# First and last steps in another order, zero matmuls and one small activation during the first loads, in a two-layer graph network kernel

## The chip, the cores and the metric

One NeuronCore of one Trainium2 chip runs the whole program. The metric is device time in microseconds (us); before the change the median of three runs is 1987.33 us. Engines are named as in the profile: PE is TensorE (PEld its weight loads), DVE is VectorE, ACT is ScalarE, POOL is GpSimd, SP is SyncE, which here only issues DMAs. An engine's queue is worked off in order; a `q` after a name (SPq) marks the sequencer that waits or issues.

## The reference

The input x is 128 batches of 128 rows and 512 columns, float32, and adj is a 128 x 128 matrix that is used as weight in layer 0 and as mask in layer 1.

```python
# layer 0: A = adj @ x, C = A + b
pre = A[:, :, None, :] + (C - A)[:, :, :, None]
out = jnp.max(jax.nn.relu(pre), axis=-1)          # = relu(max_n A + b), one number per row
x = _layernorm(x + out)
# layer 1: 8 heads of 64
qkv = x @ w_qkv
attn = softmax(where(adj == 0, -inf, q @ k.T * hd ** -0.5))
o = (attn @ v) @ w_proj + b_proj
x = _layernorm(x + (o + (layernorm(o) * ln_gamma + ln_beta)))
```

## The kernel before

Four batches make a group (32 groups), two batches a pair (64 pairs, called q or p). Per pair: layer 0 takes one 128 x 512 product with adj transposed (`l0_mm`, psum tile pa), a row maximum on DVE (`l0_max`, L267), an addition on ACT (`l0_add`, L272), statistics on DVE and POOL (`bn`, `finish_stats`: bn_stats L235, bn_aggr L236, then a small chain of POOL operations, among them a power, L246 to L248) and a normalization on ACT (`l0_norm`, `normalize`, L254). The result is transposed into x1T: for the first group by PE (`l0_transpose_pe`), for all others by DVE in blocks of 32 (`l0_transpose`) and through DRAM (`l0_write`, `l0_read`: eight DMAs of SP for each pair). `l0_beta` and `l0_spill` put x + beta away for the tail.

The big products (q and k from wqk, v from wv, o from wp) are done by Strassen's scheme in the form with seven products: a `Unit` has products 1 to 7, each of 4 matmuls, which the profile shows as 8 passes, since a float32 matmul is two. Sums of the weight blocks (`weight_sums`, POOL) and of the left blocks (`left_sums`, tiles s_x and s_o; on POOL, for the first group on DVE) feed them. Products 1, 6 and 7 add up in PSUM bank b1, product 2 goes to b2, 5 and 3 to b3, 4 to b4. `snap(k)` copies b1 to SBUF on ACT (u_qk, u_v, u_o, L173), `result(i, j)` adds a snap to a bank on DVE (L179). So product 6 waits for snap 1, product 7 for snap 2, the next unit's product 1 for snap 3, and product 3, which writes b3 after product 5, for result (1, 1).

Attention for batch b: `scores` (PE, psum tiles pss), `softmax_max` (DVE), `softmax_exp` (ACT, eight rows of operations, L400), `softmax_div` and `prob_transpose` (DVE, L411, L413, L421), through DRAM (`prob_write` one DMA, `prob_read` four, tile pT), `attend` (PE, psum po), `attend_copy` (ACT, tile oT, L471).

The tail of a batch, spread over later pairs: normalization of o (`tail_inner`, ACT), three operations on POOL (`tail_residual`: times gamma, plus o, plus the stored x), statistics, normalization (`tail_outer`, ACT) and store (SP). For the last batches there are single-row forms: `tail_inner_one`, `tail_residual_one`, `tail_outer_one`, `last_project` (a plain product with w_proj, psum tile pp), and `tail_fused`, which does inner normalization and residual in three DVE operations (L594 to L596) straight from the statistics.

All instructions are pinned in program order on each engine, so the order of the text is the order of every queue. What runs when is written out by hand: a prologue (from L612) prepares batches 0 to 9 and starts on q and k of the first group, then the loop from L706 runs pairs p = 0 to 60, and the last pairs from L860 on are written out. In the prologue, at L664 to L678, the results of the first unit stand ahead of the "second" statistics (batches 4 to 7), the sums of wv and two of the four normalizations. In the loop at p = 0 there is no attention of an earlier pair to hide behind. In the tail, L is batch 127.

Of the kernel before, what the change touches and what calls it, by code (L numbers as in the profile page):

```python
# [9 lines left out]
F32 = mybir.dt.float32  # L10
AF = mybir.ActivationFunctionType
# [5 lines left out]
def kernel(  # L17
# [30 lines left out]
    nc = tc.nc  # L48
    B, P, D = x.shape
# [3 lines left out]
    G = 4  # L53
    GT = G * P
    HT = GT // 2
    HE = D // 2
# [8 lines left out]
    const = ctx.enter_context(tc.tile_pool(name="const", bufs=1))  # L65
    sb = ctx.enter_context(tc.tile_pool(name="sb", bufs=1))
    small = ctx.enter_context(tc.tile_pool(name="small", bufs=4))
    dram = ctx.enter_context(tc.tile_pool(name="dram", bufs=3, space=bass.MemoryType.DRAM))
    psum = ctx.enter_context(tc.tile_pool(name="psum", bufs=1, space=bass.MemoryType.PSUM))

    pin = tc.keep_in_program_order

    def pe(*args, **kwargs):
        pin(nc.tensor.matmul(*args, **kwargs))  # L74
# [2 lines left out]
        pin(eng.tensor_tensor(dst, a, b, op))  # L77


    adj_sb = const.tile([P, P], F32, name="adj_sb")  # L80
    pin(nc.sync.dma_start(out=adj_sb, in_=adj))
    bias0 = const.tile([P, 1], F32, name="bias0")
# [2 lines left out]
    def broadcast(queue, name, src):  # L85
        t = const.tile([P, D], F32, name=name)
        pin(queue.dma_start(out=t, in_=src.partition_broadcast(P)))
        return t
# [26 lines left out]
    def weight_sums(w, cols, width):  # L115
        t = w[:, :, :, ds(cols, width)]
        b11, b21, b22, b12 = (t[:, i] for i in range(4))
        tt(nc.gpsimd, t[:, 4], b12, b11, ALU.subtract)
        tt(nc.gpsimd, t[:, 6], b22, b12, ALU.subtract)
        tt(nc.gpsimd, t[:, 5], b22, t[:, 4], ALU.subtract)  # L120
        tt(nc.gpsimd, t[:, 3], b21, t[:, 5], ALU.subtract)
# [3 lines left out]
    wv = const.tile([P, 7, 2, HE], F32, name="wv")  # L125
# [7 lines left out]
    weight_load(wqk, w_qkv, 0, D, HE, HE)  # L133
    load(3)

    ident = const.tile([P, P], F32, name="ident")
    make_identity(nc, ident)
    mhalf = const.tile([P, 1], F32, name="mhalf")
# [94 lines left out]
    def bn(src, mv, k):  # L233
        st = small.tile([P, 6], F32, tag="st", name=f"st_{k}_{mv.name}")
        pin(nc.vector.bn_stats(st, src))  # L235
        pin(nc.vector.bn_aggr(mv[:, k], st))  # L236

    def finish_stats(mv, keys):

        n = len(keys)  # L240
        if n == 0:
            return
        sh = small.tile([P, NC], F32, tag="sh", name=f"sh_{mv.name}")
        pin(nc.vector.tensor_scalar(sh[:, :n], mv[:, :n, 0], -1.0, None, ALU.mult))
        rs = small.tile([P, NC], F32, tag="rs", name=f"rs_{mv.name}")
        pin(nc.gpsimd.tensor_scalar(rs[:, :n], mv[:, :n, 1], EPS, None, ALU.add))  # L246
        tt(nc.gpsimd, rs[:, :n], rs[:, :n], mhalf.to_broadcast([P, n]), ALU.pow)
        tt(nc.gpsimd, sh[:, :n], sh[:, :n], rs[:, :n], ALU.mult)  # L248
        for k, key in enumerate(keys):
            stat_of[key] = rs[:, k : k + 1], sh[:, k : k + 1]  # L250
# [23 lines left out]
    def l0_norm(f):  # L274
        normalize(xs[f], xs[f], ("y", f))
# [133 lines left out]
    def softmax_div(b):  # L409
        rec = small.tile([P, H], F32, tag="rec", name=f"rec_{b}")  # L410
        pin(nc.vector.reciprocal(rec, psums.pop(b)))  # L411
        p = prob[b]
        tt(nc.vector, p, p, rec.unsqueeze(2).to_broadcast([P, H, P]), ALU.mult)  # L413
# [38 lines left out]
    def attend(b, tag="po"):  # L452
        g, h, jj = place(b)
        v, t = vs[g, h], pT.pop(b)
        pos[b] = psum.tile([P, NP, P], F32, tag=tag, name=f"po_{b}")
        for pr in range(NP):
            for par in range(2):
                pe(
                    pos[b][ds(par * HD, HD), pr],
                    lhsT=v[:, jj, ds((2 * pr + par) * HD, HD)],  # L460
                    rhs=t[:, :, par * NP + pr],
                    start=True,
                    stop=True,
                )

    def attend_copy(b):
        g, h, jj = place(b)
        if jj == 0:
            tag = "x" if (g, h) == (NG - 2, 0) else "oT"
            oT[g, h] = sb.tile([P, KC, HT], F32, tag=tag, name=f"oT_{g}_{h}", bufs=2)  # L470
        pin(nc.scalar.copy(oT[g, h][:, :, ts(jj, P)], pos.pop(b)))  # L471
# [45 lines left out]
    def o_of(b):  # L517
        g, h, jj = place(b)
        return os_[b] if b in os_ else os_[g, h][:, jj]
# [60 lines left out]
    def tail_inner_one(b):  # L580
        z_tile(b)
        normalize(zs[b], o_of(b), ("o", b))

    def tail_residual_one(b):
        tt(nc.gpsimd, zs[b], zs[b], ga_bc, ALU.mult)
        tt(nc.gpsimd, zs[b], zs[b], o_of(b), ALU.add)
        tt(nc.gpsimd, zs[b], zs[b], rs_.pop(b), ALU.add)

    def tail_fused(b, mean):

        z_tile(b)
        z, o, (rs, _) = zs[b], o_of(b), stat_of.pop(("o", b))
        stt = nc.vector.scalar_tensor_tensor
        pin(stt(z, o, mean, ga_bc, ALU.subtract, ALU.mult))  # L594
        pin(stt(z, z, rs, o, ALU.mult, ALU.add))
        tt(nc.vector, z, z, rs_.pop(b), ALU.add)  # L596

    def tail_outer_one(b):
        z = zs.pop(b)
        normalize(z, z, ("z", b))  # L600
        pin(nc.sync.dma_start(out=out[b], in_=z))

    def stats(name, *items):

        mv = small.tile([P, NC, 2], F32, tag="mv", name=f"mv_{name}")
        for k, (kind, b) in enumerate(items):
            bn({"o": o_of, "z": zs.get, "y": xs.get}[kind](b), mv, k)
        finish_stats(mv, items)
        return mv
# [4 lines left out]
    mv = [small.tile([P, NC, 2], F32, tag="mv", name=f"mv_first_{k}") for k in range(2)]  # L614
# [10 lines left out]
    weight_sums(wqk, HE, HE)  # L625
    for f in range(G):
        l0_norm(f)
    for f in range(2):
        l0_transpose_pe(f)

# [30 lines left out]
    weight_load(wp, w_proj, 0, HE, 0, HE)  # L661
    ga_bc = broadcast(nc.sync, "ga_bc", ln_gamma)
    bp_bc = broadcast(nc.sync, "bp_bc", b_proj)
    before.snap(3)  # L664
    before.result(1, 1)
    before.result(1, 0)
    stats("second", *(("y", f) for f in range(G, 2 * G)))
    weight_sums(wv, 0, HE)
    for f in range(G, G + 2):
        l0_norm(f)  # L670
    cur.product(2)
    cur.product(1)
    cur.snap(1)
    cur.result(0, 0)
    before.product(3)
    before.result(0, 1)
    for f in range(G + 2, 2 * G):
        l0_norm(f)  # L678
    cur.product(6)
    cur.snap(2)  # L680
    cur.product(5)
# [24 lines left out]
    for p in range(LAST + 1):  # L706
        g, ph = divmod(p, 2)
        a, b = 2 * p, 2 * p + 1
        first = v_unit(0) if p == 0 else qk_unit(g + 1, ph)
        n = p + 4 if p + 4 < B // 2 else None  # L710
        f = p + 5 if p + 5 < B // 2 else None
        ta, tb, to = tails(p)
        mv = small.tile([P, NC, 2], F32, tag="mv", name=f"mv_{p}")
        keys = []
# [79 lines left out]
            l0_read(n)  # L794
        if p > 0:
            first.snap(3)
        softmax_div(b)
        prob_transpose(b)
        prob_write(b)
        prob_read(a)  # L800
        prob_read(b)
        first.result(1, 1)
        first.result(1, 0)
        if ph == 1 and tb is not None:
            one("z", zs, tb)
        if ph == 0 and ta is not None:
# [13 lines left out]
        if p == 0:  # L820
            xsums = x_sums(1)
            run_sums(xsums[:3])
            second = qk_unit(1, 0)
        elif p == LAST:
            second = qk_unit(g + 1, 1)
        else:
            second = v_unit(g + 1) if ph else o_unit(g - 1)
# [32 lines left out]
    L = B - 1  # L860
# [101 lines left out]
    o_u.result(0, 0)  # L962
    v_u.product(3)
    v_u.result(0, 1)
    for t in range(L - 11, L - 7):
        tail_residual_one(t)
    o_u.product(6)
    softmax_exp(L, range(4))
# [14 lines left out]
    tail_outer(B // 2 - 7)  # L983
    tail_store(B // 2 - 7)
    mv = small.tile([P, NC, 2], F32, tag="mv", name="mv_last_2")
    keys = [("z", L - 11), ("z", L - 10), ("o", L - 5), ("o", L - 4), ("o", L - 7), ("o", L - 6)]
    bn(zs[L - 11], mv, 0)
    bn(zs[L - 10], mv, 1)
    o_u.result(1, 1)
    o_u.result(1, 0)  # L990
    bn(o_of(L - 5), mv, 2)
    bn(o_of(L - 4), mv, 3)
    o_u.product(3)
    o_u.result(0, 1)
    last_project(L - 3, wlast, "b2")
    last_project(L - 2, wlast, "pss0")
    attend(L - 1)
    attend_copy(L - 1)
    attend(L, "pa")
    attend_copy(L)  # L1000
    last_project(L - 1, wlast, "pss1")
    last_project(L, wlast, "b1")
    bn(o_of(L - 7), mv, 4)
    bn(o_of(L - 6), mv, 5)
    finish_stats(mv, keys)
    for t in (L - 5, L - 4, L - 7, L - 6):
        tail_inner_one(t)
    for t in (L - 11, L - 10):
        tail_outer_one(t)
    tail_residual_one(L - 5)  # L1010
    mv = stats("last_3", ("o", L - 3), ("o", L - 2), ("z", L - 9), ("z", L - 8))
    tail_residual_one(L - 4)
    for t in (L - 9, L - 8):
        tail_outer_one(t)
    tail_fused(L - 3, mv[:, 0, 0:1])
    tail_fused(L - 2, mv[:, 1, 0:1])
    mv = stats("last_4", ("o", L - 1), ("z", L - 3), ("z", L - 2))
    tail_residual_one(L - 7)
    tail_fused(L - 1, mv[:, 0, 0:1])
    for t in (L - 3, L - 2):  # L1020
        tail_outer_one(t)
    mv = stats("last_5", ("o", L), ("z", L - 5), ("z", L - 4))
    tail_residual_one(L - 6)
    tail_fused(L, mv[:, 0, 0:1])
    for t in (L - 5, L - 4):
        tail_outer_one(t)
    stats("last_6", ("z", L - 1), ("z", L - 7))
    stats("last_7", ("z", L), ("z", L - 6))
    for t in (L - 1, L - 7, L, L - 6):
        tail_outer_one(t)  # L1030


# [39 lines left out]
```

## Time and profile before

| What | Value |
|---|---|
| Median of three runs | 1987.33 us (1987.06 to 1987.37) |
| Profiled execution, its own time | 1988.53 us |
| Span of its instructions | 1986.7 us |
| PE busy | 1946.4 us, 98% of the span |
| DVE, POOL, ACT busy | 79%, 65%, 53% |
| Chain that ended last: PE's share | 95% |
| Mean granted TensorE clock | 0.991 |

The profile is of one execution. The span runs from its first instruction to its last; the execution's own time is 1.8 us more. "Busy" of an engine is the sum of its instructions' durations. The granted clock is the share of full speed that the chip allowed TensorE. A line of waits reads: who waited, for whom, us in total, times, longest. A line of the timeline reads: start in us from the span's start, duration, engine, line, operation, output and inputs, shape, count; in brackets the idle time of the engine before it and what ended it. A line of the chain: start, duration, what.

### The profile page before, as it was taken

The page shows a single profiled execution, that of the slowest core. Times are in us where ns is not written, and L with a number is a line of the kernel's source. Part 1 is how long each engine was busy: PE and PEld are TensorE (multiplying, and loading weights), DVE is VectorE, ACT ScalarE, POOL GpSimd, SP SyncE. Part 2 cuts the span into 40 slices and gives each one's busy share as a digit, 9 for nine tenths or more (in the row PEclk, how much of TensorE's full clock was granted, in tenths as well). Part 3 has the DMA queues.
Part 4 walks back from the last instruction along what each step waited for, and adds up shares of the span by engine and source line. Part 5 has one row for each costly group of instructions (what it writes and reads, how often), then busy time and mean ns, then how long its engine had stood idle before and what let it go on. Part 6 is the DMA issues. An engine that isn't in the chain of part 4 may idle for free.

```text
span 1986.7 us, 33036 instructions
## 1 busy us (share of the span) xinstructions
PE 1946.4 (98%) x11545; PEld 1644.8 (83%) x11545; DVE 1565.2 (79%) x2518; ACT 1055.1 (53%) x3066; POOL 1293.7 (65%) x808
## 2 busy tenths in 40 slices
PE   7999999999999999999999999999999999999994
PEld 5888888888888888888888888888888888888872
DVE  5668788788788788787787787787787787787685
ACT  3435546546556556555555555555455455455453
POOL 5246667677667677667676667676667676676646
PEclk8999999999999999999999999999999999999997
DMA  5665576675675675765766765765766766765553
GB/s 191 145 170 139 159 195 155 181 195 153 183 187 158 186 187 157 187 170 169 192 168 169 194 165 164 202 165 164 202 159 168 198 164 165 198 162 158 159 177 121
DMA packets 445655, 341.76 MB, mean 172 GB/s; under 512 B 276912, under 2 KB 378416, under 8 KB 445488
## 3 DMA queue, kind: packets, MB, share of 16 engines
q1 hardware_dynamic: 445056, 338.85, 64.1%
q8 instruction: 92, 1.51, 0.3%
q10 hardware_dynamic: 432, 0.79, 0.1%
q14 instruction: 75, 0.61, 0.1%
HBM read 172.82 MB, written 166.72 MB: 171 GB/s over the span
## 4 chain that ended last, share of the span: by engine, by line
PE 95%; DVE 2%; DMA 1%; POOL 1%; ACT 0%; issue 0%; SPq 0%; ACTq 0%; POOLq 0%; DVEq 0%
PE b_qk L74 39%; PE b_v L74 19%; PE b_o L74 19%; PE pss L74 6%; PE po L74 6%; PE pa L74 5%; PE pp L74 0%; POOL zl L77 0%; DMA x<-in_x_dram 0%; DMA wqk<-in_L_gnn_w_qkv_dram 0%; DVE s_x L77 0%; DMA hop<-pu 0%; DVE st_mv_last L235 0%; DVE z L77 0%; POOL rs_mv_last L77 0%
## 5 line engine op out<-in xcount | busy, mean ns | idle before, releaser
L74 PE MATMUL b_qk<-s_x,wqk 128*128 128x256 f32 x2048 | 476.3, 381 | 4.0 <-ACT u_qk L173 3.9
L74 PEld LDWEIGHTS b_qk<-s_x,wqk 128*128 128x128 f32 x2048 | 391.8, 191 | 58.1 <-POOL wv L77 4.3
L400 ACT ACTIVATE s<-s,nmax 128x128 f32<-128x128 f32 x1024 | 396.2, 391 | 6.7 <-DVE nmax L393 6.7
L74 PE MATMUL b_qk<-x1T,wqk 128*128 128x256 f32 x1536 | 360.7, 385 | 0.8 <-DVE x1T L299 0.8
L74 PEld LDWEIGHTS b_qk<-x1T,wqk 128*128 128x128 f32 x1536 | 288.7, 191 | 45.5 <-DVE x1T L299 1.2
L77 POOL TENSOR_TENSOR z<-z,ga_bc 128x1024 f32<-128x1024 f32 x58 | 164.6, 2838 | 168.4 <-ACT z L254 168.4
L246 POOL TENSOR_SCALAR rs_mv<-mv 128x6 f32<-128x6 f32 (+2 forms) x61 | 14.6, 240 | 380.2 <-DVE mv L236 380.2
L77 DVE TENSOR_TENSOR s<-s,rec 128x1024 f32<-128x1024 f32 x128 | 252.3, 1971 | 4.4
L173 ACT COPY u_qk<-b_qk 128x512 f32<-128x512 f32 x192 | 112.3, 585 | 248.2 <-PE b_qk L74 247.2
L74 PE MATMUL b_v<-wv,s_x 128*128 128x256 f32 x1024 | 237.2, 380 | 2.0 <-DVE v L179 2.0
L74 PE MATMUL b_o<-wp,s_o 128*128 128x256 f32 x992 | 230.2, 380 | 0.5 <-DVE v L179 0.5
L74 PEld LDWEIGHTS b_v<-wv,s_x 128*128 128x128 f32 x1024 | 194.8, 190 | 28.7 <-DVE v L179 2.4
L179 DVE TENSOR_TENSOR qk<-b_qk,u_qk 128x512 f32<-128x512 f32 x256 | 168.1, 675 | 62.2 <-PE b_qk L74 44.6
L381 DVE SCALAR_TENSOR_TENSOR s<-pss,mask 128x512 f32<-128x512 f32 x256 | 164.3, 684 | 59.5 <-PE pss L74 59.1
L74 PEld LDWEIGHTS b_o<-wp,s_o 128*128 128x128 f32 x992 | 188.5, 190 | 26.7 <-DVE v L179 0.9
L77 POOL TENSOR_TENSOR x<-x,be_bc 128x1024 f32<-128x1024 f32 x64 | 182.1, 2847 | 34.0 <-DVE rec L411 27.6
L400 ACT ACTIVATION_READ_ACCUMULATOR s<-s,nmax 128x1 f32 x1024 | 194.2, 190 | 0.0
L179 DVE TENSOR_TENSOR v<-b_v,u_v 128x512 f32<-128x512 f32 x128 | 87.0, 681 | 133.6 <-PE po L74 128.8
L173 ACT COPY u_o<-b_o 128x512 f32<-128x512 f32 x93 | 54.4, 585 | 247.3 <-PE b_o L74 247.3
L173 ACT COPY u_v<-b_v 128x512 f32<-128x512 f32 x96 | 56.2, 585 | 238.5 <-PE b_v L74 238.5
L74 PE MATMUL b_v<-wv,x1T 128*128 128x256 f32 x768 | 176.3, 379 | 0.0
L74 PEld LDWEIGHTS b_v<-wv,x1T 128*128 128x128 f32 x768 | 146.3, 190 | 31.9 <-issue 13.8
(107 smaller groups left out, 3395.5 us busy)
## 6 DMA issues: line engine op xcount, KB each, us to landing
hop<-pu SPq DMA_DIRECT2D x128, 512.0 KB, 3.5
pT<-hop SPq DMA_DIRECT2D x512, 128.0 KB, 3.7
spill<-x SPq DMA_DIRECT2D x64, 512.0 KB, 4.8
x<-in_x_dram SPq DMA_DIRECT2D x62, 512.0 KB, 4.4
xhop<-xt SPq DMA_DIRECT2D x248, 128.0 KB, 2.3
x1T<-xhop SPq DMA_DIRECT2D x248, 128.0 KB, 3.9
xr<-spill SPq DMA_DIRECT2D x59, 512.0 KB, 3.6
out_dram<-xr SPq DMA_DIRECT2D x58, 512.0 KB, 4.1
```

The source lines that it names most:

```text
L74: pin(nc.tensor.matmul(*args, **kwargs))
L77: pin(eng.tensor_tensor(dst, a, b, op))
L173: pin(nc.scalar.copy(t, self.banks[1]))
L179: nc.vector.tensor_tensor(self.out[half, col], self.banks[bank], self.snaps[k], ALU.add)
L246: pin(nc.gpsimd.tensor_scalar(rs[:, :n], mv[:, :n, 1], EPS, None, ALU.add))
L381: nc.vector.scalar_tensor_tensor(s[:, par], pss[b][par], SCALE, mask.unsqueeze(1).to_broadcast([P, NP, P]), ALU.mult, ALU.add,)
L400: nc.scalar.activation(prob[b][:, i], prob[b][:, i], AF.Exp, bias=nmax[b][:, i : i + 1], accum_out=psums[b][:, i : i + 1],)
```

## The change

It has five parts. On each engine the same work is done except for the added operations and, in the tail, two batches (L-4 and L-6) that take the fused form on DVE in place of `tail_inner_one` and `tail_residual_one`; the groups of the last statistics are cut anew.

```diff
+    zeros = const.tile([P, 2 * P], F32, name="zeros")
+    pin(nc.vector.memset(zeros, 0.0))
+    idle = psum.tile([P, 2 * P], F32, tag="b1", name="idle")
+    def keep_warm(n):
+        for _ in range(n):
+            pe(idle, lhsT=zeros[:, :P], rhs=zeros, start=True, stop=True)
...
     load(3)
+    warm = small.tile([P, 1], F32, tag="r", name="warm")
+    pin(nc.scalar.activation(warm, zeros[:, :1], AF.Identity, bias=zeros[:, :1]))
+    keep_warm(3)
     ident = const.tile([P, P], F32, name="ident")
...
     for f in range(G):
         l0_norm(f)
+    keep_warm(5)
     for f in range(2):
         l0_transpose_pe(f)
...
     bp_bc = broadcast(nc.sync, "bp_bc", b_proj)
+    stats("second", *(("y", f) for f in range(G, 2 * G)))
+    weight_sums(wv, 0, HE)
     before.snap(3)
     before.result(1, 1)
     before.result(1, 0)
-    stats("second", *(("y", f) for f in range(G, 2 * G)))
-    weight_sums(wv, 0, HE)
-    for f in range(G, G + 2):
-        l0_norm(f)
     cur.product(2)
     cur.product(1)
     cur.snap(1)
     cur.result(0, 0)
     before.product(3)
+    for f in range(G, 2 * G):
+        l0_norm(f)
     before.result(0, 1)
-    for f in range(G + 2, 2 * G):
-        l0_norm(f)
...
         if p > 0:
             first.snap(3)
+        else:
+            first.result(1, 1)
+            first.result(1, 0)
         softmax_div(b)
         prob_transpose(b)
         prob_write(b)
         prob_read(a)
         prob_read(b)
-        first.result(1, 1)
-        first.result(1, 0)
+        if p > 0:
+            first.result(1, 1)
+            first.result(1, 0)
...
-    for t in range(L - 11, L - 7):
+    for t in range(L - 11, L - 8):
         tail_residual_one(t)
...
-    keys = [("z", L - 11), ("z", L - 10), ("o", L - 5), ("o", L - 4), ("o", L - 7), ("o", L - 6)]
+    keys = [("z", L - 11), ("z", L - 10), ("o", L - 5), ("o", L - 4)]
...
     bn(o_of(L - 5), mv, 2)
     bn(o_of(L - 4), mv, 3)
+    finish_stats(mv, keys)
+    tail_inner_one(L - 5)
+    for t in (L - 11, L - 10):
+        tail_outer_one(t)
+    tail_residual_one(L - 8)
     o_u.product(3)
     o_u.result(0, 1)
     last_project(L - 3, wlast, "b2")
     last_project(L - 2, wlast, "pss0")
     attend(L - 1)
+    attend(L, "pa")
+    mv2 = stats("last_3", ("o", L - 7), ("o", L - 6), ("z", L - 9))
+    tail_inner_one(L - 7)
+    tail_outer_one(L - 9)
+    tail_residual_one(L - 5)
+    tail_fused(L - 4, mv[:, 3, 0:1])
     attend_copy(L - 1)
-    attend(L, "pa")
     attend_copy(L)
     last_project(L - 1, wlast, "pss1")
     last_project(L, wlast, "b1")
-    bn(o_of(L - 7), mv, 4)
-    bn(o_of(L - 6), mv, 5)
-    finish_stats(mv, keys)
-    for t in (L - 5, L - 4, L - 7, L - 6):
-        tail_inner_one(t)
-    for t in (L - 11, L - 10):
+    mv = stats("last_4", ("o", L - 3), ("z", L - 8), ("z", L - 4))
+    tail_residual_one(L - 7)
+    for t in (L - 8, L - 4):
         tail_outer_one(t)
-    tail_residual_one(L - 5)
-    mv = stats("last_3", ("o", L - 3), ("o", L - 2), ("z", L - 9), ("z", L - 8))
-    tail_residual_one(L - 4)
-    for t in (L - 9, L - 8):
+    tail_fused(L - 6, mv2[:, 1, 0:1])
+    mv2 = stats("last_5", ("o", L - 2), ("z", L - 6), ("z", L - 5))
+    tail_fused(L - 3, mv[:, 0, 0:1])
+    for t in (L - 6, L - 5):
         tail_outer_one(t)
-    tail_fused(L - 3, mv[:, 0, 0:1])
-    tail_fused(L - 2, mv[:, 1, 0:1])
-    mv = stats("last_4", ("o", L - 1), ("z", L - 3), ("z", L - 2))
-    tail_residual_one(L - 7)
+    tail_fused(L - 2, mv2[:, 0, 0:1])
+    mv = stats("last_6", ("o", L - 1), ("z", L - 3), ("z", L - 2), ("z", L - 7))
+    for t in (L - 3, L - 2, L - 7):
+        tail_outer_one(t)
+    mv2 = stats("last_7", ("o", L))
     tail_fused(L - 1, mv[:, 0, 0:1])
-    for t in (L - 3, L - 2):
-        tail_outer_one(t)
-    mv = stats("last_5", ("o", L), ("z", L - 5), ("z", L - 4))
-    tail_residual_one(L - 6)
-    tail_fused(L, mv[:, 0, 0:1])
-    for t in (L - 5, L - 4):
-        tail_outer_one(t)
-    stats("last_6", ("z", L - 1), ("z", L - 7))
-    stats("last_7", ("z", L), ("z", L - 6))
-    for t in (L - 1, L - 7, L, L - 6):
+    tail_fused(L, mv2[:, 0, 0:1])
+    stats("last_8", ("z", L - 1), ("z", L))
+    for t in (L - 1, L):
         tail_outer_one(t)
```

In the built program the change shows on the queues as follows. PE: three matmuls with the tile `idle` ahead of the transpose of adj, five ahead of the first `l0_transpose_pe`, and nothing else moved. DVE: one memset at the start, the four "second" statistics ahead of two results, two results of v ahead of the division of batch 1, and a new order in the tail. ACT: one activation behind the table load, the first u_qk copy of the second unit ahead of all four normalizations, and in the tail five activations ahead of the last two oT copies. POOL: six residual operations fewer, and the statistics in smaller groups. SP: the last stores in another order. GpSimd's "second" statistics and sums of wv keep their places on POOL.

## The prediction

> **What bounds the kernel now.** I read the page first, then TensorE's waits, then the granted clock by stretch, then the two ends in order of time. The page, busy time by engine and TensorE's 40 slices:
>
> ```profile
> PE 1946.4 (98%) x11545; PEld 1644.8 (83%) x11545; DVE 1565.2 (79%) x2518; ACT 1055.1 (53%) x3066; POOL 1293.7 (65%) x808
> ...
> PE   7999999999999999999999999999999999999994
> ```
>
> TensorE is the bound everywhere except in the first and the last slice. TensorE's waits from 0 to 80 us, then from 80 to 1936 us:
>
> ```profile
> PE b_qk L74 <- ACT u_qk L173: 3.9, 1, 3.9
> ...
> PE b_v L74 <- DVE v L179: 2.0, 1, 2.0
> ...
> PE b_o L74 <- DVE v L179: 0.5, 1, 0.5
> ```
>
> The loop waits 0.5 us in 1856. So a microsecond saved before 80 us stays saved to the end, and the tail's length adds directly. Granted clock (the column before the DMA share) in stretches I cut where it changes:
>
> ```profile
> 16.90:23.70 6.80, 6.02 (x21) 4.79 (x20) 1.78 (x3) 2.10 (x3) 6.64 (x8) 0.50 0.50 163
> ...
> 44.20:51.00 6.80, 5.72 (x14) 4.59 (x15) 3.69 (x6) 2.94 (x5) 6.72 (x6) 0.50 0.35 83
> ...
> 80.00:1960.00 1880.00, 1878.50 (x11285) 1596.21 (x11285) 1496.86 (x2399) 1019.66 (x2993) 1237.94 (x746) 1.00 0.65 173
> ```
>
> Half clock twice, each time 6.8 us, each time begun inside or just after a pause of TensorE (13.2 to 15.9, 41.3 to 45.3). Before 13.5 the record says 1.00, but six passes of 512 columns from 7.73 took 5.49 us, where eight take 3.70 in the tail: cold as well. The chain of waits around the second:
>
> ```profile
> 41.80 1.03 POOL rs_mv_second L77
> ...
> 43.87 0.80 ACT x L254
> 44.66 0.48 ACT u_qk L173
> 45.28 6.54 PE b_qk L74 x16
> ```
>
> ScalarE had the copy u_qk (L173) queued behind two normalizations (L254) that wait for the "second" statistics; and the 16 passes after it took 6.54 us, where 16 take 3.45 in the loop (6.91 for 32). The timeline at the other cold place, and at the end:
>
> ```profile
> 18.29 3.78 PE L74 MATMUL b_qk<-x1T,wqk 128*128 128x256 f32 x8 [0.78 <-DVE x1T L299]
> ...
> 1952.52 0.58 ACT L471 COPY oT<-po 128x512 f32<-128x512 f32 x1 [10.20 <-PE po L74]
> ...
> 1960.77 1.24 DVE L77 TENSOR_TENSOR z<-z,wlast 128x512 f32<-128x512 f32 x1
> 1961.52 1.12 PE L74 MATMUL pp<-bp_bc,ones 1*128 1x512 f32 x2
> ...
> 1982.83 0.80 ACT L254 ACTIVATE zl<-zl,sh_mv_last,rs_mv_last 128x512 f32<-128x512 f32 x1
> ```
>
> After TensorE's last matmul (1962.6) come 21 us of VectorE, GpSimd and ScalarE in turn, then 3.1 us of store.
>
> **What the Trainium skill says.** "TensorE: Matmul & The Clock Gate", Part 1: the clock is halved by default, rises after a busy window of about 3.4 us, falls after an idle one, and the window runs free. The trace agrees: both cold stretches are 6.8 us, two windows. Its Part 4 says that transposes by TensorE don't count as busy in the same way; the trace agrees insofar as eight transposes at 15.9 did not stop the fall at 16.9. "SBUF — State Buffer", Who interferes with whom: a VectorE operation with two SBUF inputs and a GpSimd operation that reads SBUF exclude each other. The trace agrees: the sums s_x on VectorE took 0.95, 1.64, 1.75 and 2.83 us beside GpSimd's, while operations with a PSUM input took 0.68 to 0.75. "ScalarE: Activation LUTs", What ACT_TABLE_LOAD costs: 1283 ns; the trace has 1.28 at 7.58.
>
> **The change, part by part** (times in the frame of before).
>
> *Three zero matmuls and the small activation at the start.* Six passes of 256 columns, cold 0.47 each (3.78/8): 2.8 us, from about 0.8 (a memset of VectorE comes first, 0.2 to 0.3 by L148 and L150) to 3.6. The adjacency transpose starts at 3.62 when its data land, so at most 0.1 is late; the next matmul that matters waits for x until 7.68. Cost 0. They could lift the clock early, but the window up to about 6.7 would be some 75% busy and no such window lifted it in before (one 69% busy, 6.7 to 10.1, did not): 0, with up to 1.2 to gain. The activation pulls the table load from 7.58 to the start; row addition 0 would be done by 8.3 instead of 9.6, but its reader, VectorE's statistics, stands behind a maximum that waits for TensorE until 9.84: 0.
>
> *Five zero matmuls after the first maxima's products.* Ten passes from 13.2, of which 0.3 us is cold (the clock rises at 13.5), then 0.216 each: done by 15.6. The first transpose waits for ScalarE until 15.91, so the cost is 0; were all ten cold, 13.2+4.7 = 17.9 and 2.0 late. The window 13.5 to 16.9 then is 60% zero matmuls where it was 28% busy. I take it that the clock stays up: the eight passes at 18.29 take 1.73, not 3.78 (2.05), the eight transposes behind them 1.72, not 1.92 (0.2). What is late next: the sums s_x on VectorE, now against GpSimd's weight sums the whole time. The second sum is done by 25.2 to 25.8 where TensorE wants it at 25.2: minus 0.3. Net gain 1.9, between −2 and 3.4.
>
> *"second" statistics and weight sums ahead of the results, normalizations behind product 3.* VectorE runs four statistics (0.83 each) first, at 33.7 to 37.0, and GpSimd has them at about 38.7. The two results (1.29), now behind them, end at 38.5; product 3, which overwrites their bank, begins at 37.7 and needs only the first, done at 37.9: 0.2, inside my rounding. On ScalarE the copy u_qk stands before the normalizations and runs at 37.8 to 38.4; the four normalizations end at 41.8; the next copy (snap 2) waits for them until 41.8, and product 7, its reader, begins at 46.3. So the 3.9 us wait goes, and with it the cold stretch: 6.54−3.45 = 3.1. Behind the normalizations stand transposes, eight writes and eight reads of SP (3.7 and 6.8 us to issue): landed at about 57 where they landed at 60.9; GpSimd's first reader, at 67.9 before, moves to 59.0. Covered by 2; without that cover each microsecond counts. Gain 7.0, between 3 and 7.
>
> *p = 0: results (1,1), (1,0) ahead of the second division.* VectorE idled 1.49 us before that division (waiting for the exponentials, 73.56 to 75.04); the two results (1.25) fit there, and TensorE finds its bank free at 76.4 instead of 78.4: 2.0. What is late next: the eight reads of pT. The last is issued at 82.7 and takes 3.7 to land: 86.45, unmoved by this edit; the second attend would start at 88.2−2.0 = 86.2. Minus 0.3. Gain 1.7.
>
> *The tail.* TensorE's order is the same. Two of the eight GpSimd residuals (three operations of 1.27 us each) become VectorE's fused form; statistics are split into smaller groups. ScalarE's two oT copies (1952.52) now stand behind five activations. These need the statistics of L−7 and L−9: GpSimd does residual L−9 by 1939.95, statistics 1942.6, residual L−8 by 1946.4, statistics 1947.9; the activations end at 1949.5. The copies' input is ready at 1952.5: 3 us of cover, cost 0. After that VectorE is the chain, from 1942.97 on. Statistics: 3+3+3+4+1+2 = 16 at 0.83, and six short ones, about 14.5. Fused on PSUM, four at 0.75+0.75+0.7 to 0.9, 9.5. Fused on SBUF, two: alone 2.1, at GpSimd's pace (three of 1.65) 4.95; GpSimd is half in short operations then, so I take 3.0 and 3.5. Sum 30.5: VectorE ends at 1973.5. Then GpSimd's three short steps 1.3, ScalarE's two rows 1.5: 1976.2 to 1976.6, against 1983.6. The store behind is as before. Gain 7.0; 3.4 for both fused at the worst pace; 9.5 at the best.
>
> **Sum.** 1.9+7.0+1.7+7.0 = 17.6. The profiled execution's span was 1986.7 and its own time 1988.5, 1.2 above the median 1987.33 of the runs. Span 1969.1, its own time 1970.9, median **1969.7 us**.
>
> **Rivals.**
> *The clock does not stay up* (zeros or 60% don't count, or the phase differs): the first 2.2 go, and up to 2.0 for cold zeros: 1972 to 1974. For: the skill on transposes. Against: the second cold stretch is then cured anyway, since no pause is left. 12%.
> *The tail's fused steps run at GpSimd's pace*, or residual L−7 becomes late: gain 3.4, 1973.3. For: s_x at 1.64 to 2.83. Against: most of GpSimd's time there is short operations. 12%.
> *The wait moves*: transposed tiles for the second group come late, and the 3.9 us come back: 1973 to 1980. For: only 2 us of cover. 7%.
> *No net change*: the tail gives nothing and the wait and cold return. Needs two failures: 4%.
> *Slower*: the pT reads. If TensorE, pulled ahead at p = 0, met them late in each of the 61 passes, a wait of 0.35 us a pass would eat 21.6 us. It decides from 0.29 us (17.6/61) on; at 0.5 the time is 2000. For: the loop's reads are the tightest transfer at p = 0 (1.8 us of cover). Against: in the loop the last read is issued by 110.8 and the attend begins at 117.2, 6.4 later, and VectorE idles 6 to 9 us of every 30, so it catches up. 4%.
>
> **Numbers.** The likeliest case has 61%, its own range 1966 to 1973 (clock up early −1.2, fused steps −2.5; s_x and rounding +3). With the clock and tail rivals the range 1965.5 to 1976.5 holds 8 in 10 and more. A difference of 0.2% (4 us) is about what can be told from none: faster 0.92, same 0.04, slower 0.04.
>
> **What would show it.** No wait of 3.9 on u_qk and no half clock at 44 to 51; granted clock 1.00 between 17 and 24; eight passes of b_qk in 1.7 us at about 18.3; no wait on v near 69; the two oT copies still released by TensorE; VectorE without a gap over 0.5 us after the last matmul, and 17 rather than 24 us from there to the end. The prediction is wrong if TensorE shows new waits in the loop, or if the fused steps L−4 and L−6 take over 5 us each.

## The result, and the profile after

The changed kernel takes 1971.99 us in the median of four runs (1970.57 to 1972.82), the kernel before 1987.35 us in four runs beside it (1987.06 to 1988.32): a ratio of 0.9921, interval 0.9904 to 0.9938. That is 15.4 us, or 0.8%, faster. The forecast was 1969.7, range 1965.5 to 1976.5. The profiled execution has a span of 1970.7 us and an own time of 1972.51, so the span is 16.0 us shorter than the one before. In the changed kernel's text the copy of a snap is line 185, a result 191, the statistics 247 and 248, the small chain behind them 256 and 258, normalization 266, the fused steps 606 and 607.

The page's busy time and TensorE's slices:

```profile
PE 1945.3 (99%) x11561; PEld 1642.2 (83%) x11561; DVE 1571.6 (80%) x2526; ACT 1054.3 (53%) x3065; POOL 1289.6 (65%) x805
...
PE   8999999999999999999999999999999999999996
```

Only the first slice (7 to 8) and the last (4 to 6) differ. TensorE's waits from 0 to 80 us, then from 80 to 1936 us:

```profile
PE pt L309 <- ACT x L266: 2.2, 1, 2.2
...
PE b_qk L74 <- DVE v L191: 0.2, 1, 0.2
...
PE b_o L74 <- DVE v L191: 0.5, 1, 0.5
```

The 3.9 us on u_qk and the 2.0 us on v are gone, and the loop has no new wait. The chain of waits where the 3.9 us stood:

```profile
38.71 5.45 PE b_qk L74 x24
44.16 1.72 PE pa L74 x4
45.87 3.45 PE b_qk L74 x16
```

TensorE runs through, 24 passes in 5.45 us at full clock. The granted clock by stretch (the column before the DMA share):

```profile
2.08:5.50 3.42, 3.04 (x7) 1.71 (x7) 0.42 (x2) 1.58 (x2) 0.00 (x0) 1.00 0.77 217
12.32:15.74 3.42, 1.21 (x8) 0.57 (x7) 2.92 (x10) 2.15 (x4) 1.56 (x5) 1.00 1.09 358
15.74:22.57 6.83, 6.05 (x19) 4.82 (x20) 1.67 (x3) 2.10 (x3) 6.67 (x7) 0.50 0.75 255
37.50:44.30 6.80, 6.77 (x31) 5.55 (x30) 5.46 (x11) 4.02 (x6) 6.12 (x7) 1.00 0.73 235
```

The second cold stretch is gone. The first is still there, as long as before: 6.83 us. The timeline of TensorE at the start shows why:

```profile
1.17 2.93 PE L74 MATMUL idle<-zeros 128*128 128x256 f32 x6 [1.17 <-DVE zeros L82]
...
7.79 2.84 PE L74 MATMUL pa<-x,adjT 128*128 128x512 f32 x6 [1.58 <-DMA x<-in_x_dram]
10.47 2.32 PE L74 MATMUL idle<-zeros 128*128 128x256 f32 x10
14.96 1.79 PE L309 MATMUL pt<-ident,x 128*128 128x128 f32 x8 [2.17 <-ACT x L266]
17.52 3.78 PE L74 MATMUL b_qk<-x1T,wqk 128*128 128x256 f32 x8 [0.78 <-DVE x1T L311]
```

The three early zero matmuls did what I had priced at nothing: the clock was up when the six row passes came (2.84 us; 5.49 before). The five later ones did not do what I had priced at 2.2: they ran at full speed, were done at 12.8, and left a gap of 2.17 us. The window from 12.32 is 35% busy (1.21 of 3.42 us), the clock fell at 15.74, and product 1 took 3.78 us as before. Other profiles agree: in all nine of kernels with the early zero matmuls the six row passes take 2.84 us, in the five of kernels without them 4.74 to 5.49; and in all six that have the five later ones and no more, product 1 takes 3.60 to 3.78 us. The tail:

```profile
1935.12 0.94 DVE L256 TENSOR_SCALAR sh_mv_last<-mv_last 128x3 f32<-128x3 f32 x1
...
1941.43 1.28 POOL L77 TENSOR_TENSOR zl<-zl,o 128x512 f32<-128x512 f32 x1
...
1941.56 1.18 DVE L256 TENSOR_SCALAR sh_mv_last<-mv_last 128x3 f32<-128x3 f32 x1
...
1942.11 0.59 ACT L483 COPY oT<-po 128x512 f32<-128x512 f32 x1 [0.46 <-PE po L74]
1942.65 0.74 DVE L606 SCALAR_TENSOR_TENSOR zl<-o,mv_last,ga_bc 128x512 f32<-128x512 f32 x1
1942.79 1.73 POOL L77 TENSOR_TENSOR zl<-zl,wlast 128x512 f32<-128x512 f32 x1
...
1943.49 1.57 DVE L607 SCALAR_TENSOR_TENSOR zl<-zl,rs_mv_last,o 128x512 f32<-128x512 f32 x1
...
1948.11 1.26 POOL L77 TENSOR_TENSOR zl<-zl,o 128x512 f32<-128x512 f32 x1
...
1948.31 1.09 DVE L256 TENSOR_SCALAR sh_mv_last<-mv_last 128x3 f32<-128x3 f32 x1
...
1951.13 1.12 PE L74 MATMUL pp<-bp_bc,ones 1*128 1x512 f32 x2
...
1966.05 1.52 ACT L266 ACTIVATE z<-z,sh_mv_last,rs_mv_last 128x512 f32<-128x512 f32 x2 [4.97 <-POOL sh_mv_last L77]
```

The last matmul ends at 1952.25, the span at 1970.7: 18.46 us, where it was 24.11. The oT copy is still released by TensorE. But three operations of 128 x 3 numbers took about 1 us each, where I had put 0.2. The chain of waits in this stretch names another engine:

```profile
1942.79 1.73 POOL zl L77
1944.51 0.65 POOL rs_mv_last L258
...
1945.25 1.29 POOL rs_mv_last L77
...
1951.01 1.36 POOL rs_mv_last L77
...
1952.40 0.76 DVE z L607
```

By this view GpSimd, not VectorE, is the chain until 1952.37; VectorE's last stretch follows. VectorE has no real gap there either (0.11 us before 1952.40): its time went into operations that took longer than their size asks.

**Where the 16.0 us of span come from** (starts of the same instruction in the two timelines, before minus after). In the kernel before:

```profile
27.31 3.69 PE L74 MATMUL b_qk<-s_x,wqk 128*128 128x256 f32 x16
...
56.82 3.62 PE L74 MATMUL b_v<-wv,x1T 128*128 128x256 f32 x16
```

In the changed kernel:

```profile
26.37 3.69 PE L74 MATMUL b_qk<-s_x,wqk 128*128 128x256 f32 x16
...
49.16 3.62 PE L74 MATMUL b_v<-wv,x1T 128*128 128x256 f32 x16
...
77.83 2.24 PE L74 MATMUL po<-pT,v 128*64 128x128 f32 x32
```

The products with the first unit's sums s_x start at 26.37 for 27.31: 0.94 from the start. The first passes of b_v start at 49.16 for 56.82, 7.66: so 6.72 from the moved statistics. The first po starts at 77.83 for 87.25, 9.42, and waits 0.26 inside itself for a pT tile: 1.5 from p = 0. The tail gives 24.11−18.46 = 5.65. That is 14.8. The other 1.2 lie between the first passes of b_o and the last projections: 1 us of it is one wait of po on a pT read in the last pairs of before's profiled execution ("PE po L74 <- DMA pT<-hop: 1.0, 1, 1.0"). No edit touches it, and the profiles of second_only, p0_only and warm_only below, which keep the old tail, don't have it. So it belongs to that one execution, and about 14.8 us are the change's.

### The profile page after: what moved, and what is told of

Its sections match the earlier page's. It is cut to its first block, busy times and chain, and to the rows that moved or that the text cites. A ratio compares the mean times of both kernels' runs of the same rounds, so it can differ in the third digit from the quotient of the medians.

```text
span 1970.7 us, 33075 instructions
## 1 busy us (share of the span) xinstructions
PE 1945.3 (99%) x11561; PEld 1642.2 (83%) x11561; DVE 1571.6 (80%) x2526; ACT 1054.3 (53%) x3065; POOL 1289.6 (65%) x805
## 4 chain that ended last, share of the span: by engine, by line
PE 95%; DVE 1%; DMA 1%; POOL 1%; ACT 1%; issue 0%; SPq 0%; ACTq 0%; POOLq 0%; DVEq 0%
PE b_qk L74 40%; PE b_v L74 19%; PE b_o L74 19%; PE pss L74 6%; PE po L74 6%; PE pa L74 5%; DMA wlast<-spill 1%; POOL zl L77 1%; DMA x<-in_x_dram 0%; DVE st_mv_last L247 0%; POOL rs_mv_last L77 0%; ACT s L412 0%; DMA hop<-pu 0%; DMA out_dram<-xr 0%; DVE amax L279 0%
## 5 line engine op out<-in xcount | busy, mean ns | idle before, releaser
L74 PE MATMUL b_qk<-s_x,wqk 128*128 128x256 f32 x2048 | 473.4, 379 | 0.3 <-DVE v L191 0.2
L74 PEld LDWEIGHTS b_qk<-s_x,wqk 128*128 128x128 f32 x2048 | 388.8, 190 | 55.0 <-issue 0.7
L74 PE MATMUL b_qk<-x1T,wqk 128*128 128x256 f32 x1536 | 360.5, 384 | 0.8 <-DVE x1T L311 0.8
L74 PEld LDWEIGHTS b_qk<-x1T,wqk 128*128 128x128 f32 x1536 | 287.8, 191 | 46.2 <-DVE x1T L311 1.2
L74 PE MATMUL b_v<-wv,s_x 128*128 128x256 f32 x1024 | 237.0, 379 | 0.0
L74 PE MATMUL b_o<-wp,s_o 128*128 128x256 f32 x992 | 230.1, 380 | 0.5 <-DVE v L191 0.5
L74 PEld LDWEIGHTS b_v<-wv,s_x 128*128 128x128 f32 x1024 | 194.4, 190 | 26.8 <-issue 0.3
L74 PEld LDWEIGHTS b_o<-wp,s_o 128*128 128x128 f32 x992 | 188.1, 190 | 27.2 <-DVE v L191 0.9
L74 PE MATMUL b_v<-wv,x1T 128*128 128x256 f32 x768 | 176.2, 379 | 0.0
L74 PEld LDWEIGHTS b_v<-wv,x1T 128*128 128x128 f32 x768 | 145.9, 190 | 32.2 <-issue 13.9
```

## The experiments

**Each part alone.** Four kernels against the kernel before (1986.72 beside them, 38 runs, 1985.6 to 1990.1).

*second_only*: only the moved statistics of the prologue.

```diff
+    stats("second", *(("y", f) for f in range(G, 2 * G)))
+    weight_sums(wv, 0, HE)
     before.snap(3)
...
     before.product(3)
+    for f in range(G, 2 * G):
+        l0_norm(f)
     before.result(0, 1)
```

> The kernel before with the 'second' statistics moved ahead of the results and the normalizations moved behind product 3, alone. My theory: the 3.9 us wait on u_qk and the half clock from 44 to 51 us go together: 7.0 us less, 1980.3 us, with the first cold stretch (16.9 to 23.7) still there. Rival: only the wait goes and the cold stretch comes at another place: 3.9 us less, 1983.4.

Measured: 1981.13 (8 runs), ratio 0.9971, interval 0.9960 to 0.9982: 5.6 us. The granted clock from 41 to 50:

```profile
41.00:50.00 9.00, 9.00 (x40) 7.17 (x39) 6.97 (x14) 4.88 (x7) 8.92 (x6) 1.00 0.76 212
```

The wait of 3.9 us and this cold stretch are gone, by this edit alone.

*p0_only*: only the two results at p = 0 ahead of the second division.

```diff
+        else:
+            first.result(1, 1)
+            first.result(1, 0)
         softmax_div(b)
```

> The kernel before with the two results of v ahead of the second division at p = 0, alone. My theory: the 2.0 us wait on v goes, 0.2 comes back at product 5 (result (0,1) stands behind the division and two maxima) and 0.3 at the second attend (pT lands late): 1.5 us less, 1985.8 us. Rival: the pT reads take all of it: 0.0 to 0.3 us less. Second rival: the loop falls behind for good: slower than before.

Measured: 1985.61 (20 runs), 0.9993, interval 0.9986 to 1.0000: 1.1 us, which the medians alone hardly tell from nothing. The profile carries it, by TensorE's waits from 0 to 80 us:

```profile
PE b_qk L74 <- ACT u_qk L173: 3.9, 1, 3.9
...
PE b_qk L74 <- DVE v L179: 0.2, 1, 0.2
```

The wait of 2.0 us on v is replaced by one of 0.2: the next result (0, 1) now stands behind the division and two maxima. The other 3.9 us is untouched.

*tail_only*: only the new tail.

```diff
-    for t in (L - 5, L - 4, L - 7, L - 6):
-        tail_inner_one(t)
...
+    tail_fused(L - 4, mv[:, 3, 0:1])
...
+    tail_fused(L - 6, mv2[:, 1, 0:1])
```

> The kernel before with the tail's new order alone. My theory: the part after TensorE's last matmul shrinks from 24.1 us to about 18.5, as in the changed kernel, and nothing else moves: 5.6 us less, 1981.7 us. Rival: the 1.03 us wait of TensorE for pT near 1939 is gone with this order too, so that 6.7 us go, 1980.6. A second rival: the tail's gain depends on the early parts (TensorE's distance to the stores and reloads), then it is under 4 us here.

Measured: 1981.57 (7 runs), 0.9975, interval 0.9964 to 0.9986: 5.2 us. From the last matmul to the end 18.73 us. The small operation of VectorE took 0.93 and 1.16 us here as well, and the chain of waits is again GpSimd's until VectorE's L595 at 1959.97. So the shortfall of the tail comes with the tail's own order, whatever stands before it.

*warm_only*: only the zero matmuls and the activation.

```diff
+    pin(nc.scalar.activation(warm, zeros[:, :1], AF.Identity, bias=zeros[:, :1]))
+    keep_warm(3)
...
+    keep_warm(5)
```

> The kernel before with the zero matmuls and the small activation alone. My theory after the first look: they lift the clock during the first products (row products at 0.43 instead of 0.86 us a pass), which brings the first normalization 0.9 us forward, but the five later ones then end 2 us before the transposes and the clock falls all the same: 0.9 us less, 1986.4 us. Rival, as predicted: the clock stays up from 13 us on and product 1 runs at 1.7 instead of 3.8 us: 1.9 us less, 1985.4. Second rival: TensorE's earlier arrival is swallowed by the 3.9 us wait at 41 to 45 us: 0.0.

Measured: 1984.53 (12 runs), 0.9988, interval 0.9979 to 0.9996: 2.2 us. TensorE's timeline:

```profile
7.33 2.84 PE L74 MATMUL pa<-x,adjT 128*128 128x512 f32 x6 [1.52 <-DMA x<-in_x_dram]
...
14.51 1.82 PE L309 MATMUL pt<-ident,x 128*128 128x128 f32 x8 [2.17 <-ACT x L266]
17.11 3.78 PE L74 MATMUL b_qk<-x1T,wqk 128*128 128x256 f32 x8 [0.78 <-DVE x1T L311]
```

Row passes at full speed, product 1 cold: the same picture as in the changed kernel. The four parts add to 5.6+1.1+5.2+2.2 = 14.1 us, against 15.4 to 16.3 for the whole on three occasions; the intervals of the parts are 2.8 to 4.4 us wide each, so they add up as far as can be told.

**What the zero matmuls do.** *no_warm* is the changed kernel without them and without the activation; *after_again* is the changed kernel beside it; *fillmid* fills the two gaps that let the clock fall:

```diff
         l0_mm(f, tag)
+        if f == 0:
+            keep_warm(2)
...
-    keep_warm(5)
+    keep_warm(8)
```

> The changed kernel once more, as the measure for the others of this call: 15 to 15.5 us less than before, about 1971.8 us.

> The changed kernel without the zero matmuls and without the small activation. My theory: what those two gave alone (2.2 us) is missing here too, since nothing later absorbs it: 1974 us, with row products at half clock. Rival: the reordered front absorbs an early or late start, then under 0.7 us is missing: 1972.3.

> The changed kernel with two more zero matmuls between the first and second row products and eight in place of five behind the fourth, so that the pauses of 1.6 and 2.2 us that were left are filled. My theory: the clock rises by 8 us and does not fall near 15.7, product 1 (eight passes at about 17.5 us) takes 1.7 in place of 3.8 us: 1.5 to 2.0 us less than the changed kernel. Rival: transposes don't hold the clock and it falls all the same: 0.0. Second rival: the fillers delay the transposes where the clock is late: 0.5 to 1.5 us more.

Measured: after_again 1970.80 (1970.36 to 1971.87), no_warm 1973.12 (1972.86 to 1975.38), fillmid 1970.18 (1969.33 to 1971.48), each four runs; before 1987.11. So the zero matmuls, with the activation, are worth 2.3 us here: the two ranges don't touch, though on other occasions the changed kernel itself ran up to 1972.8. The timeline of no_warm:

```profile
7.26 4.99 PE L74 MATMUL pa<-x,adjT 128*128 128x512 f32 x6 [0.62 <-DMA x<-in_x_dram]
15.44 1.97 PE L297 MATMUL pt<-ident,x 128*128 128x128 f32 x8 [3.19 <-ACT x L254]
18.19 3.78 PE L74 MATMUL b_qk<-x1T,wqk 128*128 128x256 f32 x8 [0.78 <-DVE x1T L299]
```

Product 1 is as cold without them as with them. What they give is the row passes, 2 us faster, and of these about 1 us arrives at the first transposes (15.44 against 14.47 in after_again). The profiled executions differ by 1.0 in span; after_again's was the slowest of its four, no_warm's the fastest, so 1.0 to 2.3 is what I can say.

The fill was run again against the changed kernel, with the activation taken out in a third kernel (*no_act*):

> The changed kernel once more, as the yardstick for the three beside it: 1970.4 to 1972.8, 15 to 16 us under before. One cold stretch of 3.4 or 6.8 us between 14 and 23, tail 18.4 after the last matmul.

> The changed kernel without the small activation at the start. My theory: worth nothing, because the table load, back at about 7.6, delays only row addition 0, whose reader on VectorE stands behind a maximum that waits for TensorE: within 0.3 us of the changed kernel, first row addition at about 8.9 and first transposes as before. Rival, the table load is on the path to the first transposes: 0.5 to 1.3 slower and transposes later by that much.

> The changed kernel with two more zero matmuls between the first and second row products and eight instead of five after the row products, once more. If the fill keeps the clock up whatever the phase of its window: no cold stretch in the record, and 1 to 2.5 us faster than the changed kernel. If it only shifts which passes run cold: within 0.5 us, and a cold stretch in the record again.

Measured, with before at 1987.74: after_third 1972.06 (1970.60 to 1972.78), no_act 1972.00 (1971.11 to 1972.47), fillmid2 1971.27 (1970.64 to 1971.64). The activation is worth nothing, as forecast, so what there is belongs to the zero matmuls. No kernel had only the three early or only the five later ones: which of them act is read from the profiles, not from times. The clock of fillmid2 by stretch:

```profile
6.20:16.00 9.80, 8.17 (x31) 5.09 (x29) 6.97 (x18) 4.30 (x6) 1.47 (x5) 1.00 1.05 361
16.00:23.00 7.00, 6.21 (x33) 5.15 (x34) 4.40 (x6) 2.11 (x3) 6.84 (x7) 1.00 0.70 235
```

and its timeline of TensorE:

```profile
17.45 1.99 PE L74 MATMUL b_qk<-x1T,wqk 128*128 128x256 f32 x8 [0.78 <-DVE x1T L311]
24.26 3.69 PE L74 MATMUL b_qk<-s_x,wqk 128*128 128x256 f32 x16 [0.32 <-DVE s_x L77]
...
77.14 1.09 PE L74 MATMUL po<-pT,v 128*64 128x128 f32 x16 [0.49 <-DMA pT<-hop]
```

In both fill kernels the profile has no cold stretch at the start, and product 1 takes 1.99 to 2.00 us. So zero matmuls do hold the clock up when they leave no gap; eight rather than five, and two in the earlier gap, were needed. But the medians gain only 0.6 and 0.8 us, and all the ranges overlap. Two of the lost parts are in the lines: the sums s_x are 0.32 late (the 0.3 I had taken off), and in fillmid2 TensorE, pulled 2.6 us further ahead (po from 75.55, where after_third has 78.12), meets the pT reads of p = 0 and waits 0.49 us. The profiled execution of after_third was the slowest of its five, that of fillmid2 the fastest of its four, so the 2.1 us between their spans is more than the kernels differ. Which of the other executions of either kernel ran cold at the start, no profile shows.

**What the small operation costs.** *sh_act* is the changed kernel with the sign change of the mean, for all statistics of the last pairs, on ScalarE; *best* is sh_act with the fill.

```diff
+        if "last" in mv.name:
+            pin(nc.scalar.activation(sh[:, :n], mv[:, :n, 0], AF.Identity, scale=-1.0))
+        else:
             pin(nc.vector.tensor_scalar(sh[:, :n], mv[:, :n, 0], -1.0, None, ALU.mult))
```

> The changed kernel with the small sign change of the tail's statistics (the operation that writes sh, three of which took 0.94 to 1.18 us on VectorE in place of 0.17) done by ScalarE instead. My theory: VectorE waits there for a GpSimd operation to end, and it is the bound of the tail together with GpSimd; without those three the tail shortens by 0.5 to 1.5 us before GpSimd's residuals take over: about 1971. Rival: GpSimd alone sets the tail, then 0.0. Second rival: ScalarE's hand-over comes late and costs 0.5 or more.

> The same fill, and in the tail the sign change of the mean on ScalarE instead of VectorE. The fill 1 to 2.5 us and the sign change 0.7 of the tail (17.74 against 18.45) add: 1.7 to 3.2 us faster than the changed kernel, tail 17.7 after the last matmul. If the sign change gains nothing in the end because GpSimd and not VectorE ends the statistics: as the fill alone, within 0.3.

Measured: sh_act 1971.57 (1971.40 to 1972.85), against 1970.80 for the changed kernel beside it; best 1970.52 (1970.01 to 1971.16), against 1972.06. In both, the tail shrank to 17.7 us from 18.4: 0.7, though the three sign changes had been 2.6 us over their price and took 0.19 to 0.21 each on ScalarE. The timeline of sh_act shows why:

```profile
1934.54 1.57 DVE L609 SCALAR_TENSOR_TENSOR zl<-o,mv_last,ga_bc 128x512 f32<-128x512 f32 x1
...
1940.83 1.81 DVE L609 SCALAR_TENSOR_TENSOR zl<-o,mv_last,ga_bc 128x512 f32<-128x512 f32 x1
```

The first step of the fused form on SBUF, which used to follow the sign change and took 0.74 us (L606), now takes 1.57 and 1.81. The third wait went in the same way to an addition z<-z,wlast, 1.54 us for 0.69. So the waits did not go: in the changed kernel the second and third sign change end within 0.03 us of the GpSimd operation of 128 x 512 numbers that ran beside them (1942.74 and 1942.71, 1949.40 and 1949.37), and when the sign change is taken away, VectorE's next operation of that kind waits instead. GpSimd's short steps stayed slow too, at 0.67 to 0.68 us for the first of the three in each group. The 0.7 that was won is about half an earlier end of this stretch by 0.3 us, and about half the two short sign changes (0.19 and 0.15) that left VectorE's last one. Yet sh_act as a whole gained nothing. The timeline of best, in the order of time, shows the cost ahead of the tail:

```profile
1906.16 2.90 PE L74 MATMUL pss<-qk 64*128 64x128 f32 x32
...
1906.20 0.21 ACT L257 ACTIVATE sh_mv_last<-mv_last 128x6 f32<-128x6 f32 x1 [4.88 <-DVE mv_last L248]
1906.31 0.57 ACT L185 COPY u_v<-b_v 128x512 f32<-128x512 f32 x1
...
1918.27 1.99 PE L74 MATMUL b_o<-wp,s_o 128*128 128x256 f32 x8 [0.85 <-DVE v L191]
```

The first of these sign changes stands on ScalarE ahead of the copy u_v, waits for the six statistics of VectorE (ScalarE idles 4.88 us), and holds up the copy by 1.9 us (its input was complete at 1904.3), the result behind it on VectorE, and the scores: 2.90 us where they take 2.06 in after_third, and a wait of 0.85 instead of 0.48. That is 1.2 us lost for 0.7 won. My edit was cut too wide. A version that moves only the three blocked sign changes was not tried. best is 1.5 us (0.08%) under the changed kernel, with ranges that overlap: no more than a hint, and as a whole it is no version that I could call better.

## Why the prediction was right, point by point

**The bound and the sign.** Right: what was saved before 80 us stayed saved. The time from the first passes of b_o to the last projections was 1805.8 us in the changed kernel and in most of the experiments, and TensorE's waits in the loop are the same 0.5 us. The slower rival (pT reads that wait in each pass) did not come; its sum, 0.35 us in 61 passes, is 21.4 us and not 21.6, which changes nothing.

**Three zero matmuls: cost 0, gain 0 to 1.2.** The step "the window up to about 6.7 would be some 75% busy" failed, on the side that I had kept open. The window that counted ran from 2.08 to 5.50 and was 89% busy (3.04 of 3.42 us). The row passes took 2.84 us, 2.65 less, and 0.94 us of that reached product 2. The gain lay towards the upper end of my bounds, where I had taken the lower.

**Five zero matmuls: 2.2 gained, 0.3 lost.** Wrong, and the step is "I take it that the clock stays up". I placed them behind cold row passes, from 13.2 to 15.6; because the three early ones worked, they ran from 10.5 to 12.8, in another window. The two steps were not independent: the success of the first took the cover of the second. no_warm shows product 1 cold without them, warm_only and the changed kernel show it cold with them, the fill shows it at 1.99 us. The mechanism was right and the amount too small. The 0.3 us on s_x appears in the fill as 0.32. Steps 1 and 2 together: 1.9 forecast, 0.94 in the profile, 2.3 in the medians of no_warm. What came near the forecast sum is luck: a gain I had put at 0 stood in for one of 1.9 that did not come. What happened to the clock here is the rival "The clock does not stay up", which had 12% and 1972 to 1974; 1971.99 lies at its edge. Two of the signs I had named, granted clock 1.00 between 17 and 24 and eight passes in 1.7 us, did not appear.

**The moved statistics: 7.0.** Right: 6.72 in the profile. The wait of 3.9 and the cold stretch went, the two results cost 0.2 at product 3 (as the forecast had it), and the copy u_qk ran ahead of the normalizations. In the medians it is 5.6 alone. A reason that the profiles speak for: the second cold stretch of the kernels that still have it was 3.4 us long in tail_only and p0_only (clock 0.81 from 41 to 50) and 6.8 us in before and warm_only. The excess it costs is 3.1 us in the longer case and, by my estimate from the lengths, about half of it in the shorter, so a median over executions is under the 7.0 of before's profile. That the length is drawn anew in each execution fits "TensorE: Matmul & The Clock Gate", Part 1 (a window of 3413 ns that runs free); four profiles can't prove it.

**p = 0: 2.0−0.3.** Right: 1.5 in the profile, 1.1 in the medians of p0_only. The pT tile was 0.26 late where I had put 0.3, but I had missed the wait of 0.24 us for result (0, 1), which I should have seen as "what is queued behind" on VectorE.

**The tail: 7.0.** Right in kind, 5.65 in size (5.2 in tail_only). The mis-sized term is "six short ones 0.2": three of them took 0.94, 1.18 and 1.09 us, 2.6 more than my 0.6. Behind it stands what the sum left out: VectorE's waits for GpSimd outside the fused steps. sh_act shows that the term is not the small operation itself, since the wait moved on to the next one. "After that VectorE is the chain" held only in part, as GpSimd's chain ran alongside to 1952.37; how the 1.35 us that are missing divide between the two is not shown. The rival "The tail's fused steps run at GpSimd's pace" did not come. The fused steps on SBUF were as I put them, 3.1 and 3.1 us for 3.0 and 3.5, and those on PSUM cheaper, 2.2 each for 2.4; so VectorE's row of operations was 32.0 us for 30.5. The row to warn me was in the trace before: of its two 128 x 2 sign changes in the tail one took 0.17, the other 0.77. And "GpSimd is half in short operations then" was a bad comfort: its short ones slow down too. By GpSimd's rows of the changed kernel's tail, grouped by shape:

```profile
L77 POOL TENSOR_TENSOR rs_mv_last<-rs_mv_last,mhalf 128x3 f32<-128x3 f32 x3 | 3.9, 1299 | 0.2
...
L258 POOL TENSOR_SCALAR rs_mv_last<-mv_last 128x3 f32<-128x3 f32 x3 | 1.6, 530 | 0.0
```

A power of three columns takes 1.30 us and an addition 0.53 in the mean, where the tail of before had 0.87 and 0.24. "SBUF — State Buffer", Who interferes with whom, says that tensor_scalar can take the port pair that VectorE and GpSimd share, and that the other engine then blocks for a whole instruction. VectorE's sign changes, which are tensor_scalar operations, fit that: they end with GpSimd's, so it seems to hold for three columns too. GpSimd's slow powers and additions fit the passage that the prediction cites, as they ran beside VectorE's operations with two SBUF inputs (1944.49 and 1945.25 beside 1943.49 and 1945.10). The cover of the oT copies was about 0.4 us (the activations ahead of them ended at 1941.7, the copy began at 1942.11), not 3, as the same waits came before it: nothing was lost, but there was little to spare.

**The sum.** 17.6 forecast: 1.9+7.0+1.7+7.0. In the profile 0.94+6.72+1.5+5.65 = 14.8; 15.4 in the medians. The 2.8 us that the profile falls short by are 1.35 in the tail, 0.96 at the start, 0.28 in the moved statistics and 0.2 at p = 0. That the total fell inside the range owes something to the early zero matmuls, which made up for part of the late ones. The 2.3 us between 1969.7 and 1972.0 in the medians are not divided further.

## What to carry to other kernels

Filler on TensorE acts on windows, not on operations: find the gap that remains when the filler itself runs at full speed, and size it for that; a filler that works moves everything behind it, other filler included. When work is moved onto VectorE while GpSimd works through large operations, price the waits of one for the other, here up to a whole operation of 1.3 us each time, and not only the operations themselves; a small operation can meet such a wait as well as a large one, and taking it away hands the wait to the next. Putting a short operation on an idle engine is free only if what it waits for is ready when its place in the queue comes.

## What the runs showed of the hardware

- A matmul of zeros counts for the clock like any other: a stretch of 3.42 us with 3.04 us busy, over half of it zeros, was followed by row passes at full speed (2.84 us for six in nine profiles, 4.74 to 5.49 in the five without). A stretch that was 35% busy was followed by half clock, so it need not be an idle one, and in the kernel before one about 70% busy (6.7 to 10.1) did not lift it. So the limit for the rise lies between 70% and 89% here, if windows begin where these stretches do.
- VectorE's sign change of 128 x 3 numbers took 0.17 to 1.18 us, and GpSimd's small steps became up to 2.8 times longer (0.24 to 0.68), beside each other's large operations. With the sign change moved away (sh_act), the fused step that followed it took 1.57 and 1.81 us for 0.74.
- On ScalarE the same sign change took 0.19 to 0.21 us in every place.
